# Attention with sigmoid scores on one core: four banks in the first sigmoid, a bank order from the middle outwards, and keys copied into their natural order

## The chip, the cores and the metric

One core of a Trainium2 chip runs the whole program. The time is the device time of one execution in microseconds (us); three executions were timed, and their median counts. One more execution was recorded by the hardware profiler; all durations below are from that one.

## What is computed

The input is x, 4 images of 64 channels by 96 x 96 pixels (N = 9216 pixels), in float32. Layer 0 normalises x in groups of two channels, makes queries and keys of 8 channels and values of 64, and adds an attention whose weights are sigmoids, not a softmax:

```python
energy = jnp.einsum('bcn,bcm->bnm', Q, K)
att = jax.nn.sigmoid(energy)
out = jnp.einsum('bcm,bnm->bcn', V, att).reshape(B, C, H, W)
out = out + x
...
scale = jax.nn.sigmoid(mlp(avg) + mlp(mx))
return out * scale[:, :, None, None]
```

Layer 1 normalises the result, takes its 2-D Fourier transform, mixes the channels of the 32 x 16 lowest modes with complex weights, and transforms back. Both layers add their input to their output. Four attention matrices of 9216 x 9216 are nearly all of the work.

## The kernel before

**Tiles.** The images are held as two pairs, `xs[0]` and `xs[1]`, with the 2 x 64 channels of a pair on 128 partitions. A pair's pixels are cut into 18 blocks of 512 queries (`NBLK`) and 72 chunks of 128 keys. A *tile* is the energies of 128 keys with 512 queries of one image; it fills one of the 8 banks of PSUM. A block has 144 tiles (`TILES`), the program 5184 (`ALL`). Tile i goes through three engines:

- TensorE (PE) multiplies 32 rows of `kT` (the keys, each split into a rounded high part and the rest so that one fp32r pass keeps the precision) with 32 rows of the block's queries (`energies`, L512). Tile i uses row group i % 4 of the array, so up to four of these matmuls run side by side. The stationary operand is 128 columns of `kT`. In `kT` the two halves h = 0, 1 of a block of keys lie interleaved, "(m h)", so these columns are every second element.
- ScalarE (ACT) takes the sigmoid of several neighbouring banks in one instruction and writes them to `at` in SBUF (`sigmoids`, L534).
- PE multiplies `at` with the values `vT` (`attend`, L551): float32, 64 columns of the array for each image of the pair, the two images side by side, accumulated over the 72 chunks in bank 7 or bank 0 (by the parity of the block).

**Bursts.** The tiles are worked in *bursts* of 7 (`SIZE`), or 6 where a bank is needed for something else. The planner (the `while len(done) < len(sizes)` loop) lists the bursts: 752 of them, 676 of 7 tiles, 74 of 6, one of 5 and one of 3. All banks but the accumulator belong to the burst, so there is no second set: the energies of the next burst go to the banks that the sigmoids of this one have read. `order[t]` is the list of banks of burst t in the order of its tiles, and the first `heads[t]` of them are read by its first sigmoid, the others by its second. Before the change `HEAD` is 3, and the order is 0 to 6 or 1 to 7, forwards or backwards by `way`.

**A step.** Step t of the main loop issues, in this order, on PE, ACT and DVE (whose order is written out by hand, `tc.manual_schedule`): the energies of burst t+1; a step of layer 1 that needs PE by itself, if one is due (`alone`; that burst has 6 tiles); the products of tiles that are left of burst t-1; the sigmoids of burst t+1; products of burst t; then, where one is due, the projections of `together[t]`; the rest of the products; then `ends[t]` (DMAs and small work on VectorE, DVE). The order on SyncE's queue (SP) and on GpSimd's (POOL) is the scheduler's.

**Projections.** `together` holds, in the first block of pair 0 (bursts 1 to 22), the projections of keys and values of the blocks that come next; in the last block of pair 0, those of pair 1; later `back_w` of layer 1. They use the banks that the first sigmoid of burst t+1 has just read, and the following burst has its order turned round (`way = -way`), so that its first energies use the other banks. `values_of(p, s)` (L446, 8 matmuls in two banks) gives values and also, in 32 more columns, queries and keys. On DVE it copies these 32 columns out (`u`, L460), then the values (`vT`, L451), then splits `u` into high and low parts (L471, L472, three times each) and transposes them (L474); four DMAs store the result in DRAM (L477).

**Where `kT` comes from.** For the first blocks (`DIRECT` = 7) `keys(0, s)` (L431, one bank) makes the keys a second time, straight in the layout of `kT`: DVE adds the bias (`full_k`, L410), rounds (`high_k`, L411) and writes `kT` (L420). For all other blocks `known_keys` (L484) reads the stored split from DRAM into `kT` with four DMAs on POOL's queue.

**Layer 1 of pair 0** runs beside the attention of pair 1, in the `alone` steps and the later `together` steps; the first two of them compute the channel gate (`hidden`, `gates`: DVE `gsum` L596, ACT `gate` L597). Layer 1 of pair 1 follows after the last burst. Neither is touched.

## Time and profile before

| | |
|---|---|
| three timed executions | 3073.45, 3070.55, 3075.11 us (median 3073.45) |
| profiled execution | 3069.26 us, of which the profile's span is 3067.5 us |
| granted TensorE clock | 0.997 |
| PE busy | 3045.5 us (99%) |
| ACT busy | 2418.7 us (79%) |
| DVE busy | 313.2 us (10%) |
| POOL busy | 84.4 us (3%) |
| products, L551 on PE | 11832 matmuls, 2401.8 us busy |
| energies, L512 on PE | 5184 matmuls, 571.9 us busy |
| sigmoids, L534 on ACT | 676 of four banks, 1.872 us each; 826 of three, 1.451 us each; one of two |

Stages by the table of windows (PE busy out of the stretch, in us): first block 94.75 of 98.80 (from 26.3), the other blocks of pair 0 up to the projections of pair 1 1278.67 of 1278.90 (from 125.1), those projections 120.90 of 121.00 (from 1404), attention of pair 1 with layer 1 of pair 0 824.64 of 825.00 (from 1525), attention of pair 1 alone 627.88 of 628.00 (from 2350), layer 1 of pair 1 80.63 of 89.00 (from 2978).

How to read it: PE is the row of matmuls, PEld that of the weight loads, which run beside the matmuls. PE counts as busy while a matmul is under way, also while it fills or drains, so 99% does not say that PE streams at its full rate; the distances between starts of instructions tell more. In a row of the timeline the first number is the start, the second the length, and the square bracket holds the idle time before it with what ended it. DVE and ACT may be idle without cost as long as nobody waits for them.

### The profile page before, as it was taken

Reading aid. Unit: us, or ns where it says so; the run is one execution under the profiler, and the core shown is the slowest. Engines: PE = TensorE matmul, PEld = TensorE weight load, DVE = VectorE, ACT = ScalarE, POOL = GpSimd, SP = SyncE. Lnnn points to the kernel's source line nnn. Section 1 sums busy time; section 2 is a strip of 40 time slices with the busy share of each in tenths; the row PEclk is TensorE's granted clock in tenths of the full one; section 3 lists DMA queues with packets and bytes.
Section 4 is the critical chain, followed back from the end, with each engine's and each line's share of the span. In section 5 each row is a group of like instructions: output and inputs, shape, how many; then the busy total and the mean of one; then the engine's idle time right before and its main releaser. Section 6 shows DMA issues by size and latency. Waiting matters only on the chain.

```text
span 3067.5 us, 43100 instructions
## 1 busy us (share of the span) xinstructions
PE 3045.5 (99%) x18772; PEld 1152.3 (38%) x18772; DVE 313.2 (10%) x731; ACT 2418.7 (79%) x1543; POOL 84.4 (3%) x168
## 2 busy tenths in 40 slices
PE   8999999999999999999999999999999999999998
PEld 4433333333333333334433333333333333333336
DVE  6300000000000000002411101000000000000005
ACT  4788888888888888887788887777778888888872
POOL 0200000000000000001200000000001000000001
PEclk9999999999999999999999999999999999999998
DMA  5100000000000000001322322321113000000027
GB/s 175 41 4 4 4 4 4 4 3 4 2 4 4 4 4 4 4 4 37 84 74 71 82 78 87 131 34 32 50 50 125 4 4 4 4 4 4 5 63 248
DMA packets 122285, 119.42 MB, mean 39 GB/s; under 512 B 83664, under 2 KB 93648, under 8 KB 122000
## 3 DMA queue, kind: packets, MB, share of 16 engines
q1 hardware_dynamic: 110080, 87.69, 10.1%
q0 software_dynamic: 9488, 24.26, 2.4%
q10 hardware_dynamic: 2528, 4.72, 0.4%
q8 instruction: 147, 2.41, 0.3%
q14 instruction: 42, 0.34, 0.0%
HBM read 80.50 MB, written 34.93 MB: 38 GB/s over the span
## 4 chain that ended last, share of the span: by engine, by line
PE 97%; DVE 1%; DMA 1%; issue 0%; ACT 0%; SPq 0%; POOL 0%; DVEq 0%; POOLq 0%; ACTq 0%
PE banks L551 75%; PE banks L512 17%; PE banks L446 1%; PE banks L209 1%; PE banks L379 1%; PE py L1003 0%; PE pv L209 0%; PE pa L905 0%; DMA x<-in_x_dram 0%; ACT at L534 0%; PE banks L357 0%; PE idle_I-15339_15354 L868 0%; SPq L477 0%; PE pu L917 0%; PE banks L305 0%
## 5 line engine op out<-in xcount | busy, mean ns | idle before, releaser
L534 ACT ACTIVATE at<-banks 128x1536 f32<-128x1536 f32 x1503 | 2396.0, 1640 | 559.3 <-PE banks L512 527.2
L551 PE MATMUL banks<-at,vT 128*64 128x512 f32 (+1 forms) x11832 | 2401.8, 546 | 0.0
L551 PEld LDWEIGHTS banks<-at,vT 128*64 128x64 f32 x11832 | 781.2, 136 | 1347.8 <-issue 1294.7
L512 PE MATMUL banks<-q,kT 32*128 32x512 f32 x5040 | 551.2, 458 | 0.5
L512 PEld LDWEIGHTS banks<-q,kT 32*128 32x128 f32 x5040 | 239.0, 190 | 450.5 <-ACT at L534 332.2
L557 DVE SCALAR_TENSOR_TENSOR x<-banks,x 128x512 f32<-128x512 f32 x36 | 24.9, 692 | 2006.0 <-PE banks L551 1930.7
L484 POOL DMA_DIRECT2D kT<-qk x116 | 57.4, 502 | 943.2 <-DMA qk<-turned 892.3
L446 PEld LDWEIGHTS banks<-cs,x 128*64 128x64 f32 x576 | 39.9, 139 | 17.0 <-issue 8.8
L446 PE MATMUL banks<-cs,x 128*64 128x160 f32 (+1 forms) x576 | 45.4, 299 | 0.0
L382 DVE TENSOR_TENSOR x<-banks,x 128x384 f32<-128x384 f32 x24 | 13.4, 557 | 196.6 <-PE banks L379 191.8
L149 POOL TENSOR_TENSOR mr_l<-ve_l,cs 128x1 f32<-128x1 f32 x4 | 2.2, 561 | 839.4 <-DVE ve_l L148 839.4
L559 DVE TENSOR_REDUCE maxs<-x 128x1 f32<-128x512 f32 x36 | 24.7, 686 | 1.2
L512 PE MATMUL banks<-q_first,kT 32*128 32x512 f32 x144 | 20.7, 475 | 4.1 <-DVE vT L451 2.4
L451 DVE TENSOR_TENSOR vT<-banks,cs 128x512 f32<-128x512 f32 x36 | 24.5, 680 | 0.0
L472 DVE TENSOR_TENSOR t<-u,t 128x64 fp32r<-128x64 f32 x105 | 23.5, 226 | 3.5
L656 DVE COPY ws<-banks 128x512 f32<-128x512 f32 x16 | 11.1, 692 | 116.3 <-PE banks L209 108.6
L565 DVE BATCH_NORM_STATS2 stats<-x 128x6 f32<-128x512 f32 x36 | 22.2, 679 | 5.7 <-DMA x<-in_x_dram 5.4
L474 DVE STREAM_TRANSPOSE turned<-t 128x384 f32<-128x384 f32 x35 | 20.7, 590 | 1.2
L890 POOL DMA_DIRECT2D x<-vT x3 | 2.7, 989 | 647.9 <-DVE less L880 647.9
L656 DVE COPY ae<-banks 128x512 f32<-128x512 f32 x6 | 4.1, 691 | 157.7 <-issue 115.6
L604 PE MATMUL banks<-x 128*128 128x256 f32 (+1 forms) x44 | 14.1, 470 | 5.8 <-DMA x<-in_x_dram 5.8
L379 PE MATMUL banks<-cs,ws 128*64 128x384 f32 x96 | 19.6, 486 | 0.0
(132 smaller groups left out, 447.8 us busy)
## 6 DMA issues: line engine op xcount, KB each, us to landing
ws<-in_spec_dram SPq DMA_DIRECT2D x20, 512.0 KB, 5.8
q<-qk SPq DMA_DIRECT2D x280, 32.0 KB, 1.8
x<-in_x_dram SPq DMA_DIRECT2D x14, 512.0 KB, 8.4
qk<-turned SPq DMA_DIRECT2D x140, 48.0 KB, 2.0
room<-in_spec_dram SPq DMA_DIRECT2D x12, 512.0 KB, 5.1
w<-in_spec_dram POOLq DMA_DIRECT2D x10, 512.0 KB, 6.8
old<-in_x_dram SPq DMA_DIRECT2D x12, 384.0 KB, 4.6
x1d<-x SPq DMA_DIRECT2D x12, 384.0 KB, 3.4
```

The source lines that it names most:

```text
L209: self.last = nc.tensor.matmul(pv[bass.ts(g, 32), :].rearrange("q (n k o) -> q n k o", n=SIDE, o=C)[:, :, k, :], self.ut[:, at:at + 32], s ...
L379: nc.tensor.matmul(py[bass.ts(b, C), :4 * W], self.z[:, i, bass.ts(b, C)], named("gw"), start=True, stop=True)
L446: projected[0] = nc.tensor.matmul(pp[bass.ts(e, P // 2), h, a, :], src[:, a, h, bass.ts(e, P // 2)], named("wv")[:, :width], start=True, s ...
L451: nc.vector.tensor_tensor(vT[:, 4 * s:4 * s + 4, :].rearrange("p (h a) m -> p h a m", h=2), pp[:, :, :, :P], named("bv").unsqueeze(1).unsq ...
L472: nc.vector.tensor_tensor(to[:, 1], whole, to[:, 0].bitcast(F32), ALU.subtract)
L484: nc.gpsimd.dma_start(kT[bass.ts(r, QK), s, :].bitcast(F32), split[p][s][:, r % 2, bass.ts(r // 2, NB // 2)])
L512: nc.tensor.matmul(banks[:, bank_of(i), :], kT[r:r + 32, i % TILES // 8, :].rearrange("r (m h) -> r h m", h=2)[:, i // 4 % 2], ask[i // TI ...
L534: nc.scalar.activation(at[:, of:of + n, :], banks[:, bank:bank + n, :], AF.Sigmoid)
L551: attended[0] = nc.tensor.matmul(acc[half, cols], vT[:, j, half], at[:, place(2 * pair + b), cols], start=(j == 0), stop=(j == NCH - 1 and ...
L557: nc.vector.scalar_tensor_tensor(blk, acc, 1.0, blk, ALU.mult, ALU.add, accum_out=sums[p][:, m:m + 1])
L559: mark[0] = nc.vector.tensor_reduce(maxs[p][:, m:m + 1], blk, AX.X, ALU.max)
L565: each = [lambda s=s: nc.vector.bn_stats(stats[:, s, :], xs[p][:, bass.ts(s, NB)]) for s in range(NBLK)]
```

## The change

- `HEAD` goes from 3 to 4: the first sigmoid of a burst takes four banks and the second the other three (two in a burst of 6). Where one to three banks of the burst are lent to projections (56 bursts), the first sigmoid keeps three.
- A new function `bank_order` puts four middle banks (3 to 6, or 4 to 7; mirrored where `way` is negative) first. `way` is turned only after projections, no longer set anew at the end of each block, so that the same banks come first before and after a block's end.
- `DIRECT` goes from 7 to 9: the keys of blocks 7 and 8 are projected by `keys`, too. `values_of(0, s)` is issued up to one burst earlier (`5 * SIZE` for `4 * SIZE`).
- `kT` is stored with the halves one after the other, "h m". `keys` writes `full_k` in that order. `known_keys` loads into a buffer `come`, and a DVE copy, two steps later (`arrive`), puts it into `kT`.
- In a step with projections DVE now empties the banks first (`full_k`, `u`, `vT`); rounding, splitting, the write to `kT` and the transpose follow behind the rest of the step's products (`rest`, `put_by`).

The number of bursts, their sizes and the steps with layer 1 stay as they were.

```diff
-SIZE, HEAD = 7, 3
-DIRECT = 7
+SIZE, HEAD = 7, 4
+DIRECT = 9
...
-        kT = kvp.tile([P, NBLK, NB // 2], F32R, tag="kT", name="kT")
+        kT = kvp.tile([P, NBLK, 2, P], F32R, tag="kT", name="kT")
...
-            ku, kh = halves(pp[:, :NB // 2], named("bk"), f"k_{p}_{s}")
-            low_or_high(kT[:, s, :], ku, kh, low_sb[:, 1:2])
+            shape = [P, NB // 2]
+            u = qp.tile(shape, F32, tag="turned", name=f"full_k_{p}_{s}")
+            nc.vector.tensor_scalar(u.rearrange("p (h m) -> p m h", h=2),
+                                    pp[:, :NB // 2].rearrange("p (m h) -> p m h", h=2),
+                                    named("bk"), None, ALU.add)
+
+            def rest():
+                h = qp.tile(shape, F32R, tag="t", name=f"high_k_{p}_{s}", bufs=1)
+                nc.vector.tensor_copy(h, u)
+                low_or_high(kT[:, s, :, :].rearrange("p h m -> p (h m)"), u, h, low_sb[:, 1:2])
+            return rest
...
         def known_keys(p, s):
 
+            come = work.tile([P, STRIP], F32, tag="old", bufs=2, name=f"come_{p}_{s}")[:, :NB // 2]
             for r in range(4):
-                nc.gpsimd.dma_start(
-                    kT[bass.ts(r, QK), s, :].bitcast(F32),
-                    split[p][s][:, r % 2, bass.ts(r // 2, NB // 2)])
+                nc.gpsimd.dma_start(come[bass.ts(r, QK), :],
+                                    split[p][s][:, r % 2, bass.ts(r // 2, NB // 2)])
+            return lambda: nc.vector.tensor_copy(
+                kT[:, s, :, :], come.rearrange("p (m h) -> p h m", h=2))
...
-                                 kT[r:r + 32, i % TILES // 8, :].rearrange(
-                                     "r (m h) -> r h m", h=2)[:, i // 4 % 2],
+                                 kT[r:r + 32, i % TILES // 8, i // 4 % 2, :],
...
+        def arrive(t, p, s):
+            come = []
+            end(t, lambda: come.append(known_keys(p, s)))
+            end(t + 2, lambda: come[0]())
...
+        def bank_order(few, odd, n):
+
+            if way < 0:
+                odd = not odd
+            if few:
+                a = [4, 5, 6, 3, 2, 1]
+            elif not odd:
+                a = [4, 5, 6, 3, 2, 1, 0]
+            elif 0 < n < HEAD:
+                a = [5, 6, 7, 4, 3, 2, 1]
+            else:
+                a = [4, 5, 6, 7, 3, 2, 1]
+            return a if way > 0 else [7 - bank for bank in a]
...
-            free = range(1, 7) if few else range(7) if block[t] % 2 == 0 else range(1, 8)
-            if crossing:
-                way = 1 if n % 2 else -1
-            elif together.get(t - 1):
+            if together.get(t - 1):
                 way = -way
-            heads.append(max(HEAD, sum(size for size, _ in together.get(t, ()))))
-            order.append(list(free)[::way][:ALL - total[t]])
+            beside = sum(size for size, _ in together.get(t, ()))
+            heads.append(HEAD - 1 if 0 < beside < HEAD else HEAD)
+            order.append(bank_order(few, block[t] % 2, beside)[:ALL - total[t]])
...
-                i = 0
+                i, put_by = 0, []
                 for size, step in together.get(t, ()):
+                    if size == 2 and i > 1:
+                        put_by.pop(0)()
                     spare[0] = min(order[t + 1][i:i + size])
                     i += size
+                    put_by += [step() or (lambda: None)]
+                attend(items[at_work:])
+                for step in put_by:
                     step()
-                attend(items[at_work:])
```

## The prediction

> **What bounds the kernel now.** I read the page's head first, then the chain, then the timeline burst by burst. Head and chain (share of the span by engine, then by line):

> ```profile
> span 3067.5 us, 43100 instructions
> PE 3045.5 (99%) x18772; PEld 1152.3 (38%) x18772; DVE 313.2 (10%) x731; ACT 2418.7 (79%) x1543; POOL 84.4 (3%) x168
> ...
> PE 97%; DVE 1%; DMA 1%; issue 0%; ACT 0%; SPq 0%; POOL 0%; DVEq 0%; POOLq 0%; ACTq 0%
> ```

> PE sets the end, DVE and ACT only where PE waits for them. The question is what a burst of 7 tiles takes and what sets that. I call the start of a burst's first key-weight load its start, and the distance to the next one its period. 604 of the 752 bursts have 7 tiles and nothing beside them; their median period is 3.829 us, and in sum they are only 9.5 us above 604 times that. So almost nothing is lost there, unless the 3.829 us themselves can shrink. One number tempts: ACT's two sigmoids take 3.22 us together and start 0.61 us after the burst, 3.83 in all; and the fourth key-weight load (its bank comes free with the second sigmoid) stands at 55 to 63 ns, not at 10. That is the wait which a first sigmoid of four banks removes. Two neighbouring bursts from the timeline of weight loads (start, length, idle before it):

> ```profile
> 304.47 0.32 PEld L512 LDWEIGHTS banks<-q,kT 32*128 32x128 f32 x7 [0.39 <-ACT at L534]
> 305.14 0.63 PEld L551 LDWEIGHTS banks<-at,vT 128*64 128x64 f32 x8 [0.36 <-issue]
> ...
> 308.30 0.31 PEld L512 LDWEIGHTS banks<-q,kT 32*128 32x128 f32 x7 [0.81 <-issue]
> 308.97 0.14 PEld L551 LDWEIGHTS banks<-at,vT 128*64 128x64 f32 x2 [0.36 <-issue]
> ```

> In the first the second sigmoid was done 108 ns early and the fourth load stood at 10 ns; in the second it stood at 62. Energies to products takes 0.67 us in both, and the periods are 3.832 and 3.828. The loads of the second round stand at 115 to 120 ns anyway, and behind them the wait disappears. The steady burst is PE's own: 7 x 0.427 = 2.99 us of products, 0.43 of energies, 0.41 of filling and draining at the two changes.

> **Part 1, four banks first: 0 in the steady burst.** One burst of before has a first sigmoid of four (its steps lend four banks): it starts at 628 ns, not 614. The second then ends at 0.628 + 3.22 = 3.85 us, 20 ns into the next burst; the fifth load gets its release near 70 ns, ahead of its 115. Gain 0, loss 0.

> **A real gain: late second sigmoids, -3.2.** After a burst of 6, two old tiles are left, and the second sigmoid of the next burst waits until PE has read their places in `at`:

> ```profile
> 297.28 1.45 ACT L534 ACTIVATE at<-banks 128x1536 f32<-128x1536 f32 x1 [0.60 <-PE banks L512]
> 298.94 1.88 ACT L534 ACTIVATE at<-banks 128x2048 f32<-128x2048 f32 x1 [0.21 <-PE banks L551]
> ...
> 300.87 0.20 PEld L512 LDWEIGHTS banks<-q,kT 32*128 32x128 f32 x4 [0.18 <-ACT at L534]
> ```

> It starts 2.27 us into its burst instead of 1.96, ends late, and holds four loads of the next burst until 376 ns; that period is 3.978. With four banks first the second sigmoid starts at 0.628 + 1.77 = 2.40, past the wait, and ends at 3.85. I count 15 such bursts at about 0.14 us and 14 at 0.08 (loads at 313 to 320): 3.2 us, between 0 and 3.6. Ten more at 0.25 us stay: there a full burst's sigmoids meet a period of only 3.40, and 3 or 4 banks first give the same end.

> **Bank order, `way`: 0.** Only at 4 places does a first sigmoid now wait for an old tile (at most 0.5 us each). A block's end in before shows DMA waits for the new queries (0.07 to 0.17 us each), which stay.

> **Natural order of `kT`: 0, bounds -6.8 and 0.** The nearest rows are loads of 128 columns with unit stride (L905, L868): their second load follows after 107 ns, that of `kT` (four loads at once) after 115 to 116. If all 9 ns were the stride, 751 x 9 ns = 6.8 us would go. I take 0: L446 loads every second element, too, and takes 139 ns against 137 of L379. [...]

> **Part 2, emptying banks first: +4.2.** The line-up of DVE in a step with both projections, before:

> ```profile
> 62.25 0.48 DVE L410 TENSOR_SCALAR full_k<-banks,cs 128x256 f32<-128x256 f32 x1 [0.83 <-issue]
> 62.77 0.29 DVE L411 CAST high_k<-full_k 128x256 fp32r<-128x256 f32 x1
> 63.09 0.48 DVE L420 SCALAR_TENSOR_TENSOR kT<-high_k,cs,full_k 128x256 fp32r<-128x256 f32 x1
> 63.50 0.28 DVE L460 TENSOR_TENSOR u<-banks,cs 128x128 f32<-128x128 f32 x1
> 63.70 0.68 DVE L451 TENSOR_TENSOR vT<-banks,cs 128x512 f32<-128x512 f32 x1
> ```

> `kT` is ready at 63.58, 4.66 us into its burst (start 58.92); the burst lasts 5.34 without waits (3.83 + 1.085 values + 0.43 keys). After the change, DVE takes `full_k`, waits for the values' matmuls (their end + 0.28 us, 4.24 us into the burst), takes `u` and `vT` (0.21 + 0.68), then L411 and L420 (0.8): `kT` at 5.86 + 0.06, or 0.43 more where the projections come half a pair later. The very next burst needs these keys, at tile 4, 5, 6, 0, 1, 2, 3 for blocks 2 to 8. A wait of L costs L at tiles 0 to 2, and L - 0.24 from tile 3 on (the loads held until 1287 and 2094 ns in before cost 1.05 and 1.87). Against the waits that stand there in before: +0.57, +0.30, +0.58, +0.83, +0.58, +1.01, +0.34 = 4.2. What the early emptying frees is covered by these same waits. Bounds 0 (if the order hid itself) and 7 x 1.0.

> **Part 3, `come` copies: +5.65.** In the built instruction order the copy stands on DVE behind the transpose of step t + 2. With values alone, `u` begins 3.85 or 4.25 us into the burst in turn, the transpose ends 2.6 later, and the copy (0.29 as L411, 0.48 as L410; I take 0.3) is done and seen at `u` + 2.9: 6.75 or 7.15, where the next burst starts at 4.92. Blocks 9, 10, 11 are used by just that next burst (tiles 4, 5, 6): waits of 2.25, 1.85, 2.25, less 0.24: 2.0 + 1.65 + 2.0. From block 12 on, a burst more lies between, and the copy is early. Bounds 0 and 3 x 2.4. The 18 copies of pair 1 (some 15 bursts ahead) cost PE nothing; if that cover went, 0.3 us each.

> **DMA waits that go: -4.95.** In before, keys of block 7 and on arrive late by DMA:

> ```profile
> 83.43 0.31 PEld L512 LDWEIGHTS banks<-q_first,kT 32*128 32x128 f32 x5 [0.39 <-ACT at L534]
> 84.90 0.38 PEld L512 LDWEIGHTS banks<-q_first,kT 32*128 32x128 f32 x2 [1.17 <-DMA kT<-qk]
> ```

> Against its undisturbed 4.92 (with values) or 3.83, bursts 8, 11, 14, 17, 18 are longer by 0.36, 1.43, 0.82, 0.98, 1.27, three others by 0.03 each. Block 7 becomes direct, the copies replace 9 to 11, and from 12 on the values come a burst earlier: the chain from the transpose's end to the landed keys (91.7 to 100.6, 8.9 us: SP's four DMAs, then POOL's four) is over before the copy's turn, by about 1 us. Bounds -4.95 and -2.95 (that hand lost on the last bursts).

> **Two more key projections: +0.86** (2 x 0.43 on PE).

> **The gate, +1.7.** The last two copies of pair 1 stand on DVE ahead of `gsum`, which ACT's `gate` and every sigmoid behind it wait for:

> ```profile
> 1518.27 1.96 POOL L484 DMA_DIRECT2D kT<-qk  x4 [2.73 <-PE banks L551]
> 1520.40 0.16 DVE L596 TENSOR_REDUCE gsum<-banks 128x1 f32<-128x2 f32 x1 [6.82 <-PE banks L593]
> ```

> The last of these four DMAs lands near 1521.8, so `gsum` moves from 1520.4 to about 1522; bounds 0 and 2.5. [...]

> **Sum**: -3.2 + 4.2 + 5.65 - 4.95 + 0.86 + 1.7 = +4.3 us. On the profiled execution 3069.26 becomes 3073.5; on the median, 4.2 above it, 3073.45 becomes **3077.7**, 0.14% longer. About 0.2% (6.1 us) is what a measurement of this kernel tells from no change: below 3067.3 is faster, above 3079.6 slower.

> **Rivals.** (a) *The fourth load paces the burst after all.* ACT's 3.83 equals the period, which speaks for it; the pair at 304 and 308 speaks against. Up to 50 ns x 604 = 30 us: 3047. (b) *Slower: DVE's queue waits for DMAs.* A copy that is not landed holds the next `u` and `vT`. It decides once the chain of 8.9 us exceeds about 11.8 (9.8 for two steps, 2 until the next `u`); then each of some 23 copies costs the excess, 0.6 us each being 14: 3090. POOL's issues of 0.5 us and the two `come` buffers speak for it, the 1 us in hand against. (c) *The first block's waits go without the new ones* (DVE less late than I sum): -4.95 + 0.86 - 3.2 = -7.3: 3066. That the steady state doesn't change at all is my forecast.

> **How the numbers follow.** Forecast 0.60 (0.40 within 0.2%, 0.20 slower, for its bounds reach +14.6); (a) 0.10, faster; (b) 0.15, slower; (c) 0.15 (0.09 faster, 0.06 within). Faster 0.19, same 0.46, slower 0.35. The low bounds of all terms sum to -6.8 - 3.6 - 4.95 + 0.86 = -14.5 (3059), the high ones to 7 + 7.2 - 2.95 + 0.86 + 2.5 = +14.6 (3088). This range leaves out (a) and half of (b), about 0.18.

> **What would show it.** Right: periods of plain bursts stay at 3.83, loads of bursts 10 to 12 wait for DVE's `kT` copy near 2 us, bursts 6 and 7 for the `kT` that L411 of the changed kernel writes, second sigmoids no longer wait for PE at 300 us, `gsum` starts behind the last `come` copy. Wrong: a plain period below 3.82, or bursts 14 to 18 still waiting.

## The result and the profile after

The changed kernel takes 3073.31 us (median of 12 executions, 3071.9 to 3075.25), the kernel before, timed beside it, 3072.89 us (12 executions, 3068.29 to 3075.11). The ratio is 1.0003, with a 95% interval of 0.9994 to 1.0011: no change that this measurement can tell. In us the interval is -1.8 to +3.4; the median of 3077.7 us that was forecast, 4.2 us above that of before, was not met. The profiled execution took 3073.33 us with a span of 3071.2, where that of before took 3069.26 with 3067.5. Head and chain of the page after:

```profile
span 3071.2 us, 43088 instructions
PE 3040.2 (99%) x18780; PEld 1137.4 (37%) x18780; DVE 323.6 (11%) x764; ACT 2412.0 (79%) x1543; POOL 80.9 (3%) x160
...
PE 96%; DVE 2%; ACT 1%; DMA 1%; issue 0%; SPq 0%; POOL 0%; DVEq 0%; ACTq 0%; POOLq 0%
```

PE is 5 us less busy in a span that is 3.7 us longer, and DVE now ends some of its waits (2% of the chain for 1%). So the change gained and lost at once. Summed by kinds of burst from the starts of the first key-weight loads, after less before, in us (a plain burst is one with nothing beside it):

| part of the span | bursts | after less before |
|---|---|---|
| first block (bursts 0 to 21) | 22 | +7.55 |
| plain bursts, no wait in either | 545 | -4.20 |
| bursts with a wait in before (late second sigmoids, last bursts of a block) | 57 | -4.42 |
| bursts with a wait only in after | 5 | +1.08 |
| bursts behind a block's end or beside layer 1 | 95 | -1.75 |
| projections of pair 1 (355 to 377) | 23 | +0.55 |
| the gate (378 to 381) | 4 | +4.49 |
| ahead of burst 0 and behind the last | | +0.43 |
| sum | | +3.73 |

The plain burst, from the timeline of weight loads of the changed kernel (start, length, idle before it):

```profile
300.43 0.31 PEld L518 LDWEIGHTS banks<-q,kT 32*128 32x128 f32 x6 [0.39 <-issue]
...
303.82 0.30 PEld L518 LDWEIGHTS banks<-q,kT 32*128 32x128 f32 x7 [0.38 <-issue]
...
307.64 0.30 PEld L518 LDWEIGHTS banks<-q,kT 32*128 32x128 f32 x7 [0.81 <-ACT at L539]
```

The median period of plain bursts is 3.822 us where it was 3.829. The fourth load now stands at 10 ns (56 before), the fifth at 108 (116 before). The loads from 300.43 on wait for no late sigmoid any more.

In the first block the copies hold the keys, as the prediction had it. Weight loads of bursts 10 and 11 of the changed kernel:

```profile
85.82 0.19 PEld L518 LDWEIGHTS banks<-q_first,kT 32*128 32x128 f32 x4 [0.81 <-issue]
87.97 0.19 PEld L518 LDWEIGHTS banks<-q_first,kT 32*128 32x128 f32 x3 [1.96 <-DVE kT L491]
92.64 0.29 PEld L518 LDWEIGHTS banks<-q_first,kT 32*128 32x128 f32 x5 [0.39 <-issue]
94.36 0.18 PEld L518 LDWEIGHTS banks<-q_first,kT 32*128 32x128 f32 x2 [1.43 <-DVE kT L491]
```

DVE's line-up in the step of burst 5 (to be read beside the one in the prediction) has turned round: the values first, then `kT`. The copy of `full_k` alone also takes 0.69 us instead of 0.48; it now changes the order of the columns (in the run without copies, below, where it does not, it takes 0.48 again).

```profile
60.45 0.69 DVE L427 TENSOR_SCALAR full_k<-banks,cs 128x256 f32<-128x256 f32 x1 [2.50 <-PE banks L422]
61.47 0.29 DVE L460 TENSOR_TENSOR u<-banks,cs 128x128 f32<-128x128 f32 x1 [0.34 <-PE banks L446]
61.68 0.68 DVE L451 TENSOR_TENSOR vT<-banks,cs 128x512 f32<-128x512 f32 x1
62.28 0.28 DVE L433 CAST high_k<-full_k 128x256 fp32r<-128x256 f32 x1
62.60 0.48 DVE L411 SCALAR_TENSOR_TENSOR kT<-high_k,cs,full_k 128x256 fp32r<-128x256 f32 x1
```

At the gate, `gsum` starts behind the last copy, 6.5 us later in the span and 2.6 us later within its burst:

```profile
1526.71 0.29 DVE L491 CAST kT<-come 128x256 fp32r<-128x256 f32 x1 [5.56 <-DMA come<-qk]
1526.91 0.15 DVE L601 TENSOR_REDUCE gsum<-banks 128x1 f32<-128x2 f32 x1
```

One thing stood in no step of the prediction. The table of windows of the changed kernel, cut at the times at which the granted clock changes (length, busy time and number of PE, PEld, DVE, ACT, POOL, then the granted clock, DMA share, GB/s):

```profile
53.24:56.65 3.41, 2.04 (x15) 0.96 (x15) 3.17 (x14) 1.51 (x2) 0.00 (x0) 1.00 0.13 26
56.65:60.06 3.41, 3.41 (x12) 1.20 (x10) 1.30 (x3) 1.82 (x1) 0.00 (x0) 0.50 0.34 78
...
1527.79:1531.21 3.42, 2.03 (x13) 0.82 (x13) 3.37 (x5) 3.42 (x3) 0.00 (x0) 1.00 0.86 295
1531.21:1534.62 3.41, 3.41 (x10) 0.97 (x8) 1.88 (x3) 1.99 (x2) 0.00 (x0) 0.50 0.86 297
```

Twice PE waited for about 1.4 us of a window of 3.41 us, and twice the next window ran at half clock. PE is "busy" through all of it, at half the pace: in the first of these half-clock windows the pairs of weight loads of the products begin 0.85 us apart (56.85 and 57.70), in plain bursts 0.43. Burst 5 lasts 9.88 us, of which some 1.7 are this. The first of the two waits is not new. In burst 5 the last loads wait for the copy of the values (L451) out of the banks, until 2.09 us into the burst here and 2.10 in before, and before has 1.46 us of idle PE in one window there, without a half-clock window behind it. The loads of after, then the loads and that window of before:

```profile
55.41 0.18 PEld L518 LDWEIGHTS banks<-q_first,kT 32*128 32x128 f32 x2 [1.80 <-DVE vT L451]
...
53.80 0.20 PEld L512 LDWEIGHTS banks<-q_first,kT 32*128 32x128 f32 x4 [1.90 <-DVE vT L451]
...
50.26:53.68 3.42, 1.96 (x23) 1.26 (x19) 3.17 (x12) 1.36 (x1) 0.00 (x0) 1.00 0.19 45
```

### The profile page after: what moved, and what is told of

Same layout as the page of the kernel before. It is cut to its first block, busy times and chain, and to the rows that moved or that the text cites. A ratio compares the mean times of both kernels' runs of the same rounds, so it can differ in the third digit from the quotient of the medians.

```text
span 3071.2 us, 43088 instructions
## 1 busy us (share of the span) xinstructions
PE 3040.2 (99%) x18780; PEld 1137.4 (37%) x18780; DVE 323.6 (11%) x764; ACT 2412.0 (79%) x1543; POOL 80.9 (3%) x160
## 4 chain that ended last, share of the span: by engine, by line
PE 96%; DVE 2%; ACT 1%; DMA 1%; issue 0%; SPq 0%; POOL 0%; DVEq 0%; ACTq 0%; POOLq 0%
PE banks L556 75%; PE banks L518 16%; PE banks L446 1%; ACT at L539 1%; PE banks L209 1%; PE banks L379 1%; PE py L1029 0%; PE pv L209 0%; DMA x<-in_x_dram 0%; PE pa L931 0%; PE banks L357 0%; PE idle_I-15399_15414 L894 0%; DVE vT L451 0%; PE pu L943 0%; PE banks L305 0%
## 5 line engine op out<-in xcount | busy, mean ns | idle before, releaser
L539 ACT ACTIVATE at<-banks 128x2048 f32<-128x2048 f32 (+1 forms) x1503 | 2389.2, 1640 | 587.1 <-PE banks L518 560.1
L518 PE MATMUL banks<-q,kT 32*128 32x512 f32 x5040 | 542.8, 452 | 4.1 <-ACT at L539 3.9
L518 PEld LDWEIGHTS banks<-q,kT 32*128 32x128 f32 x5040 | 223.8, 182 | 451.4 <-issue 325.7
L562 DVE SCALAR_TENSOR_TENSOR x<-banks,x 128x512 f32<-128x512 f32 x36 | 24.9, 692 | 1994.5 <-PE banks L556 1994.5
L489 POOL DMA_DIRECT2D come<-qk x108 | 53.8, 505 | 951.0 <-DMA qk<-turned 896.7
L446 PEld LDWEIGHTS banks<-cs,x 128*64 128x64 f32 x576 | 40.0, 139 | 16.3 <-issue 11.2
L446 PE MATMUL banks<-cs,x 128*64 128x160 f32 (+1 forms) x576 | 45.4, 299 | 0.0
L451 DVE TENSOR_TENSOR vT<-banks,cs 128x512 f32<-128x512 f32 x36 | 24.5, 680 | 0.0
L474 DVE CAST t<-u 128x64 fp32r<-128x64 f32 x105 | 19.6, 189 | 0.2
```

The costliest lines, as they stand in the source:

```text
L446: projected[0] = nc.tensor.matmul(pp[bass.ts(e, P // 2), h, a, :], src[:, a, h, bass.ts(e, P // 2)], named("wv")[:, :width], start=True, s ...
L451: nc.vector.tensor_tensor(vT[:, 4 * s:4 * s + 4, :].rearrange("p (h a) m -> p h a m", h=2), pp[:, :, :, :P], named("bv").unsqueeze(1).unsq ...
L489: nc.gpsimd.dma_start(come[bass.ts(r, QK), :], split[p][s][:, r % 2, bass.ts(r // 2, NB // 2)])
L518: nc.tensor.matmul(banks[:, bank_of(i), :], kT[r:r + 32, i % TILES // 8, i // 4 % 2, :], ask[i // TILES][r:r + 32, :], start=True, stop=True)
L539: nc.scalar.activation(at[:, of:of + n, :], banks[:, bank:bank + n, :], AF.Sigmoid)
L562: nc.vector.scalar_tensor_tensor(blk, acc, 1.0, blk, ALU.mult, ALU.add, accum_out=sums[p][:, m:m + 1])
```

## The experiments

Each run is compared with executions of the kernel before that were timed beside it on the same chip; their medians were 3069.72 to 3070.13 us, where that of the result is 3072.89, so ratios are to be compared, not times. "First block" is the sum of bursts 0 to 21 from the run's trace, 110.28 us before and 117.83 after.

Each trace is of one execution, and the waits for keys out of DRAM differ from one execution to the next. The run with stalls, below, has the same code up to burst 29 as the run with both edits, and yet its first block took 110.22 us for 111.93: burst 8 took 5.18 us for 6.09, burst 11 4.91 for 6.40, burst 15 6.42 for 4.91, while bursts 2 to 7 agree to 0.01 us. So a difference of 1 to 2 us in bursts of the first block that wait for DMAs is not shown by one pair of traces.

### Four banks first, alone

The kernel before with `HEAD = 4` and `bank_order`:

```diff
-SIZE, HEAD = 7, 3
+SIZE, HEAD = 7, 4
...
-            heads.append(max(HEAD, sum(size for size, _ in together.get(t, ()))))
-            order.append(list(free)[::way][:ALL - total[t]])
+            beside = sum(size for size, _ in together.get(t, ()))
+            heads.append(HEAD - 1 if 0 < beside < HEAD else HEAD)
+            order.append(bank_order(few, block[t] % 2, beside)[:ALL - total[t]])
```

> The kernel before with the four-bank first sigmoid and the middle-out bank order alone (keys, their storage, DVE's order and the DMAs as before). Theory A (the prediction): the steady burst is PE's own, so plain bursts keep their 3.829 us though the fourth load now stands at 10 ns, the fifth stays at 115 to 116, and only the late second sigmoids go: about -3.0 us, some 3070 us, with nothing lost in the first block. Theory B: the fourth load at 10 ns instead of 56 is what made plain bursts of the changed kernel 7 ns shorter: period 3.822 here, -5 more, about -8 us, 3065. Either way the step of the gate (bursts 378 to 380) shows whether four banks first cost something there by themselves: about +1.5 us by the first sigmoid that stood at 2.2 us in the changed kernel, 0 if all of that loss comes from the copies.

3067.33 us, ratio 0.9992 (0.9983 to 1.0000). Two neighbouring plain bursts of this run:

```profile
302.74 0.31 PEld L512 LDWEIGHTS banks<-q,kT 32*128 32x128 f32 x7 [0.81 <-ACT at L534]
...
306.57 0.32 PEld L512 LDWEIGHTS banks<-q,kT 32*128 32x128 f32 x7 [0.39 <-issue]
```

The fourth load stands at 10 ns in the median, the fifth at 115, and the median period is 3.830: theory A holds, theory B is out. Bursts that waited in before lose 4.09 us, those behind a block's end or beside layer 1 another 0.98; five bursts with new waits take back 1.09 and the projections of pair 1 0.75: -3.2 us. The gate costs 1.25 us by itself, as the changed kernel's first sigmoid at 2.2 us into burst 378 had hinted. Contrary to both theories, the first block grew by 1.99, of which 1.68 are a half-clock window in burst 5.

### Unit stride, alone

The kernel before with chunks of neighbouring pixels; the same in the split and in DRAM, and no copy:

```diff
-        src = xs[p][:, bass.ts(s, NB)].rearrange("p (a m h) -> p a h m", a=2, h=2)
+        src = xs[p][:, bass.ts(s, NB)].rearrange("p (a h m) -> p a h m", a=2, h=2)
...
-                    split[p][s].rearrange("r k (a g m) -> g r (k a) m", a=2, g=4)[g],
-                    turned[bass.ts(g, QK)].rearrange("r k a m -> r (k a) m"))
+                    split[p][s].rearrange("r k (a h g m) -> g r (k a h) m", a=2, h=2, g=4)[g],
+                    turned[bass.ts(g, QK)].rearrange("r k a (h m) -> r (k a h) m", h=2))
...
-                                 kT[r:r + 32, i % TILES // 8, :].rearrange(
-                                     "r (m h) -> r h m", h=2)[:, i // 4 % 2],
+                                 kT[r:r + 32, i % TILES // 8, bass.ts(i // 4 % 2, P)],
```

> The kernel before with three banks first, and unit stride in kT got without any copy: a chunk is 128 neighbouring pixels, in the values, in the split and in kT (the transposed split is stored in DRAM in runs of 32 elements instead of 64). Theory A (the prediction): the stride of the key weights costs nothing, plain bursts stay at 3.829 and the time at about 3073. Theory B': unit stride takes 7 to 8 ns from the second round of key-weight loads (fifth load at 108 instead of 116), and from every burst: period 3.822, some 715 bursts, -5 us, about 3068. The finer runs in DRAM can make the keys of blocks 7 and on land later in the first block: 0 to +2 us.

3064.57 us, ratio 0.9982 (0.9973 to 0.9991). The row of the key-weight loads among the costliest groups of before, then of this run; the last number ahead of the second bar is the mean length of one in ns:

```profile
L512 PEld LDWEIGHTS banks<-q,kT 32*128 32x128 f32 x5040 | 239.0, 190 | 450.5 <-ACT at L534 332.2
...
L512 PEld LDWEIGHTS banks<-q,kT 32*128 32x128 f32 x5040 | 228.1, 182 | 450.9 <-ACT at L533 323.8
```

With four banks first it is 190 ns as well. The fourth load still stands at 60 ns, the fifth at 108, the period is 3.822: theory B' holds, -4.29 us in the 550 plain bursts and -1.3 in the others behind the first block. The first block is 0.37 us longer (burst 8 alone +0.53); that the finer runs in DRAM delay its keys is not shown, since that burst differs by 0.91 us between two executions of the same code.

### Both

> Both of the former edits on the kernel before, without the late splits, the copies and the two more key projections. If the terms add up: -3.0 (late second sigmoids) and -5.0 (unit stride) and 0 to +2 (finer runs in DRAM, gate), so about 3066 us, faster than both kernels; plain period 3.822. If the fourth load and the stride share one limit, no more than the better of the two alone.

3062.21 us, ratio 0.9976 (0.9967 to 0.9985): faster than both kernels. The terms add up: plain bursts -4.25, bursts that waited -4.40, the gate +1.23, the first block +1.65 (no half clock in it; 1.04 of it is burst 19, whose loads wait for sigmoids that started only 3.3 us into burst 18, the second with four banks first behind bursts with three).

### Splitting at once

The changed kernel with the rest of each projection issued right behind its first copies:

```diff
-                    put_by += [step() or (lambda: None)]
+                    (step() or (lambda: None))()
+                    put_by.append(lambda: None)
```

> The changed kernel, with the rest of each projection (rounding, the write to kT, splitting, transposing) issued on DVE right behind its first copies, as before the change; copies by way of come, nine direct blocks and unit stride stay. The prediction's term for the emptying is 4.2 us, all of it in bursts 2 to 8, where kT waits for the values: by it about 3069 us, and bursts 2 to 8 together 4 to 6 us shorter than in the changed kernel (46.69 us), with bursts 10 to 12 unchanged (6.83, 6.39, 6.83). Rival: the keys are late because the queue of DVE is full there in either order, and no more than 1 us comes back.

3069.92 us, ratio 1.0001 (0.9992 to 1.0010), so by time alone nothing can be told. By the traces the rival (no more than 1 us comes back) is out: bursts 2 to 9 take 47.28 us, not 51.86: 4.58 less, of which 1.7 are the half clock of burst 5 that is not there, and 2.9 the emptying. But bursts 10 to 12 take 21.78 instead of 20.04, because here burst 10 is the one that ran at half clock:

```profile
80.50:83.91 3.41, 1.76 (x13) 0.58 (x11) 2.92 (x11) 1.45 (x1) 0.00 (x0) 1.00 0.16 35
83.92:87.33 3.41, 3.41 (x14) 1.24 (x11) 0.00 (x0) 1.88 (x1) 1.96 (x4) 0.50 0.47 96
```

### No copy

The changed kernel with unit stride by the layout, as above, and keys loaded straight into `kT`:

```diff
-            come = work.tile([P, STRIP], F32, tag="old", bufs=2, name=f"come_{p}_{s}")[:, :NB // 2]
             for r in range(4):
-                nc.gpsimd.dma_start(come[bass.ts(r, QK), :],
-                                    split[p][s][:, r % 2, bass.ts(r // 2, NB // 2)])
-            return lambda: nc.vector.tensor_copy(
-                kT[:, s, :, :], come.rearrange("p (m h) -> p h m", h=2))
+                nc.gpsimd.dma_start(
+                    kT[bass.ts(r, QK), s, :, :].rearrange("p h m -> p (h m)").bitcast(F32),
+                    split[p][s][:, r % 2, bass.ts(r // 2, NB // 2)])
+            return lambda: None
```

> The changed kernel without the copies: chunks of neighbouring pixels as in the unit-stride run, keys loaded by DMA straight into kT; four banks, nine direct blocks and late splitting stay. The prediction put the copies at +5.65 us in bursts 10 to 12 and +1.7 at the gate; the trace of the changed kernel has waits of 2.16, 1.72 and 2.16 us there, and gsum 2.6 us late and, in the very next window, a half clock that cost some 1.7 us more. Theory: without the copies bursts 10 to 12 last some 4.9 us each (5 to 5.6 us less in sum), bursts 378 to 380 lose only what four banks first cost there (1.3 us, as in both runs with four banks on the kernel before), no half clock behind the gate; 0 to +2 us come back as DMA waits because the runs in DRAM are finer. About 3065 where the changed kernel would be at 3070 on this chip. Rival: without the copy the waits for the DMAs of before come back in full (4.95 us), and the time stays within 2 us of the changed kernel.

3062.78 us, ratio 0.9977 (0.9968 to 0.9986). Bursts 10 to 12 take 15.01 us (20.04 with the copies), with waits of no more than 0.2 us:

```profile
89.45 0.57 PEld L515 LDWEIGHTS banks<-q_first,kT 32*128 32x128 f32 x7 [0.39 <-issue]
94.51 0.46 PEld L515 LDWEIGHTS banks<-q_first,kT 32*128 32x128 f32 x7 [0.81 <-issue]
```

So the copies cost 5.0 us there. The gate costs 1.23 us instead of 4.49, and no half clock follows it: the copies' share is 3.26, of which 1.7 are the half clock and some 1.55 the late `gsum`. The rival (DMA waits come back in full) is out.

### Values early, on the fast kernel; three banks behind projections

On the run with both edits, first the values one burst earlier, then also three banks first in the two bursts behind values:

```diff
-                while (valued < min(NBLK, (total[t] + 4 * SIZE - 1) // 8 + 1)
+                while (valued < min(NBLK, (total[t] + 5 * SIZE - 1) // 8 + 1)
...
             beside = sum(size for size, _ in together.get(t, ()))
+            if any(sum(size for size, _ in together.get(t - k, ())) > 1 for k in (1, 2)):
+                beside = max(beside, 1)
```

> Four banks and unit stride on the kernel before, and the values issued up to one burst earlier, as in the change, with seven direct blocks and no copies. The prediction's term for DMA waits that go was -4.95, of which the changed kernel showed -0.8, -1.0, -0.6 at bursts 14, 17, 18. Theory: an earlier burst of values takes bursts 11, 14, 17 and 18 of the run with both edits (6.41, 5.70, 4.45 and 5.31 us) to 4.9, 4.9, 3.9 and 4.5: -3 to -4 us, about 3058 to 3059. Rival: SP's queue of stores (23 us without a pause in that run) is what makes the keys late, and an earlier start moves the waits to other bursts: within 1 us of that run.

> The run before this one, with three banks first in the two bursts behind each step with values (seven bursts change, two of them at the gate, bursts 377 and 378, the others in the first block). In all kernels with four banks first the first sigmoid of burst 378 waits to 2.2 us into its burst until PE has read its places in at; with three it stood at 0.67. Theory: bursts 377 to 380 come back to the 18.9 us of the kernel before, 1.3 us less, and the first sigmoid of the burst behind the projections of the first block stands at about 0.65, not at 1.4 to 3.3: -1.3 to -2 us in all. Rival: the second sigmoid waits instead, and nothing changes.

3061.90 us, ratio 0.9971 (0.9959 to 0.9983), and 3061.72 us, 0.9972 (0.9961 to 0.9983). Earlier values leave bursts 11, 14 and 18 at 4.91, 4.95 and 3.82 us, at or below what their theory had, and burst 17 at 4.88, where 3.9 was expected. The first block is 3.56 us shorter than in the trace of the run with both edits, but only 1.84 shorter than in that of the run with stalls, which has the same code there, so the size of the gain is not shown; 1.27 are lost again in the bursts with `back_w`, where the bank order comes out mirrored, and the times cannot tell the run from that with both edits (ratio 0.9976): the 3058 to 3059 us of the theory were not reached. The second run is a miss: burst 378 falls from 4.46 to 3.82 us, but 379 to 381 grow from 11.47 to 13.35, with first sigmoids at 2.0 and 2.6 us into bursts 379 and 380; in the first block burst 17 gains 1.05 and bursts 19 and 20 lose 1.75. It is not the second sigmoid that waits, as its rival had it, but the first one of the first bursts with four banks behind those with three: the wait moves with that border, and nothing is won.

### Stalls on purpose

The run with both edits, and in 43 plain bursts of pair 0 one tile's sigmoid made 1 to 6 times more:

```diff
+                    for _ in range(dose.get(t + 1, 0)):
+                        of, bank, _ = next(parts(t + 1))
+                        nc.scalar.activation(at[:, of, :], banks[:, bank, :], AF.Sigmoid)
                     sigmoids(t + 1)
```

> The run with both edits, with stalls put in on purpose: in 43 plain bursts of pair 0 ACT makes the sigmoid of the burst's first tile 1 to 6 times more ahead of its two sigmoids (7 or 8 bursts for each number, some 0.6, 1.1, 1.6, 2.1, 2.6 and 3.1 us). Theory: PE waits that long, and in addition, where PE is idle for more than some 1.35 us of one of the 3.41 us windows on which the granted clock changes, the next window runs at half clock and costs another 1.7 us: none of the 22 short stalls, some 60% at 1.6, 75% at 2.1, all above 2.6, so about 25 half windows and 75 + 43 us in all, near 3175 us. Rival: the half clock at burst 5 and at the gate is not due to PE's waits: no half windows here beyond those of that run, near 3135 us.

One execution: 3183.37 us. By the number of extra sigmoids:

| extra sigmoids | stalls | PE idle, us | followed by half clock | time lost, without / with half clock, us |
|---|---|---|---|---|
| 1 | 8 | 0.19 | 0 | 0.46 / - |
| 2 | 7 | 0.81 | 0 | 1.09 / - |
| 3 | 7 | 1.37 | 2 | 1.72 / 3.42 |
| 4 | 7 | 2.00 | 4 | 2.33 / 4.07 |
| 5 | 7 | 2.60 | 7 | - / 4.57 |
| 6 | 7 | 3.27 | 7 | - / 5.60 |

The theory holds, the rival (3135 us, no half windows) is out; 20 half windows came where about 25 were expected. The half-clock windows begin at whole multiples of 3.413 us from each other. What decides in these stalls is how much of one falls into a single window. Two stalls of four extra sigmoids, each with 2.0 us of idle PE, in the table of windows:

```profile
685.95:689.36 3.41, 1.41 (x11) 0.38 (x7) 0.00 (x0) 3.41 (x3) 0.00 (x0) 1.00 0.00 0
689.37:692.77 3.40, 3.40 (x11) 1.01 (x10) 0.00 (x0) 2.65 (x2) 0.00 (x0) 0.50 0.00 0
883.92:887.33 3.41, 2.43 (x12) 0.57 (x8) 0.00 (x0) 3.31 (x4) 0.00 (x0) 1.00 0.00 0
887.33:890.74 3.41, 2.40 (x15) 0.98 (x17) 0.00 (x0) 3.41 (x4) 0.00 (x0) 1.00 0.00 0
890.75:894.15 3.40, 3.40 (x27) 1.36 (x25) 0.00 (x0) 2.25 (x2) 0.00 (x0) 1.00 0.00 0
```

The first lies in one window, and the next has half clock; the second is split 0.98 to 1.01 over two, and nothing follows. Of the stalls whose largest share of a window was 1.32 us or less (22) none was followed by half clock, of those with 1.37 or more (21) all but one (at 1.46).

### No copy and splitting at once

The changed kernel with the edits of both runs ("both undone" in what follows): what stays are four banks, bank order, unit stride, nine direct blocks and the earlier values.

> The changed kernel without the copies (as in the run without copies) and without the late splits (as in the run with splits at once): what stays of the change is four banks first, the bank order, unit stride by the layout, nine direct blocks and the earlier values. If the two terms add up: bursts 2 to 9 as in the run with splits at once (2.9 us less than in the changed kernel, half clocks aside), bursts 10 to 12 at about 5 us each as in the run without copies, the first block some 2 us shorter than before, no half clock behind burst 5; about 3059 to 3060, the fastest so far. Rival: with the splits back at once, the stores of the split start earlier but the values' banks are free later, and the two cancel: the time of the run without copies, 3062.8.

3058.83 us, ratio 0.9961 (0.9947 to 0.9975), the fastest here. The first block takes 107.14 us, no half clock lies in the attention, and DVE's share of the chain is back at 1%:

```profile
span 3057.1 us, 43055 instructions
...
PE 97%; DVE 1%; ACT 1%; issue 0%; DMA 0%; SPq 0%; POOL 0%; DVEq 0%; ACTq 0%
```

The first block of five kernels, in us (half-clock windows in brackets):

| bursts | before | after | no copy | split at once | both undone |
|---|---|---|---|---|---|
| 0, 1 | 7.35 | 7.54 | 7.34 | 7.53 | 7.34 |
| 2 to 9 | 45.87 | 51.86 (1) | 51.87 (1) | 47.28 | 46.49 |
| 10 to 12 | 15.16 | 20.04 | 15.01 | 21.78 (1) | 14.94 |
| 13 to 21 | 41.91 | 38.39 | 38.38 | 38.39 | 38.37 |
| sum | 110.28 | 117.83 | 112.61 | 114.99 | 107.14 |

### Stride four

The changed kernel with the keys of two neighbouring blocks interleaved in `kT`, 16 bytes from column to column:

```diff
-        kT = kvp.tile([P, NBLK, 2, P], F32R, tag="kT", name="kT")
+        kT = kvp.tile([P, NBLK // 2, P, 2, 2], F32R, tag="kT", name="kT")
...
-                                 kT[r:r + 32, i % TILES // 8, i // 4 % 2, :],
+                                 kT[r:r + 32, i % TILES // 16, :, i // 8 % 2, i // 4 % 2],
```

> The changed kernel with the keys of two neighbouring blocks interleaved in kT as well, so that the 128 columns of a chunk stand 16 bytes apart (every fourth element) instead of next to each other; the copies on DVE write them so. Only plain bursts are to be read (the bookkeeping of waits sees two blocks as one, so the first block and the projections of pair 1 may lose some us). Theory: a key-weight load takes longer with the stride, 7 to 9 ns for each doubling: fifth load at 122 to 125 ns, plain period 3.836 to 3.840, 11 us or more on the whole. [...] Rival: the gain of unit stride comes from something else in that layout (the values' loads, the banks): plain period 3.822 as in the changed kernel.

One execution: 3168.22 us. Loads of a plain burst and the group's row:

```profile
1254.70 0.54 PEld L520 LDWEIGHTS banks<-q,kT 32*128 32x128 f32 x7 [0.39 <-issue]
```

```profile
L520 PEld LDWEIGHTS banks<-q,kT 32*128 32x128 f32 x5040 | 400.7, 313 | 447.6 <-issue 304.2
```

The fifth load stands at 212 ns and the period is 3.947, so neither the theory (122 to 125 ns, 3.836 to 3.840) nor the rival (3.822) holds. What a doubling of the distance costs is not one number: the fifth load comes 8 ns later from one element to two, and 96 ns later from two to four; a load takes 182 ns on average in the changed kernel (one element), 190 in before (two) and 313 here (four).

| distance of the columns | fifth load, ns | period, us |
|---|---|---|
| 1 element | 108 | 3.822 |
| 2 elements | 116 | 3.829 |
| 4 elements | 212 | 3.947 |

## Why the prediction came out as it did

The forecast of no measurable change held. On the pair of profiled executions even the size fits: +4.3 us was summed, they differ by 4.07. But that fit is in good part luck. The timed medians differ by 0.42 us only, and in the traces two errors took each other away: a gain that was put at 0 and two windows of half clock that were in no term.

- **Four banks first: right in the steady burst and for the late sigmoids.** 0 in the steady burst, with the fourth load at 10 ns and no change (first run), so rival (a) is out. In that run the 24 bursts that no longer wait for a late second sigmoid gave 2.9 us, where 3.2 were summed.
- **Bank order and block ends, 0: wrong on both sides.** In the same run the 33 last bursts of a block, whose waits were to stay, gave 3.2 us; why they got shorter no run separates. On the other side 11 bursts grew by 2.3 us, the projections of pair 1 by 0.75 and the gate by 1.25. That all but the gate nets to some -3 us, like the term for the sigmoids alone, is luck.
- **Natural order of `kT`, 0: wrong.** It gave 4.2 us in the plain bursts, 5.6 in all when done alone. The bounds held the value, the choice within them did not. I had the right nearest row (second loads with unit stride, at 108 to 109 ns in the trace, not 107 as I wrote) and set it aside for one that is farther: L446 has the stride and takes no longer. In the unit-stride run L446 takes 139 ns with unit stride as well, so that row says nothing against a gain: its loads have 64 columns, on all rows of the array at once, and are not four on four row groups. The claim that the steady burst is PE's own was right and too short: the rate at which key weights come in is part of it (8 ns at the fifth load, 7 in the period). Its products stand 0.429 us apart in the trace of before, 3.00 for seven, where 0.427 and 2.99 were taken; the split of the rest into energies, filling and draining was an estimate, which no run takes apart.
- **Emptying banks first, +4.2: right in kind, somewhat large.** 2.9 us (after against split at once) and 3.7 (no copy against both undone), half clocks left out. The waits for the `kT` of L411 stand in bursts 4, 7, 8 and 9 (loads at 921, 490, 922 and 490 ns); in burst 6 they are only 39 ns, since burst 5 ran long. The slower `full_k` (0.69 for 0.48 us) was not in the sum: it adds 0.2 us to each of bursts 2, 4 and 6 in the run with splits at once, where that of both undone has none.
- **`come` copies, +5.65: right.** The loads waited until 2155, 1721 and 2155 ns, where 2.25, 1.85 and 2.25 us were worked out; 5.0 us.
- **DMA waits that go, -4.95: right, somewhat large.** Without copies, bursts 11, 14, 17 and 18 are 1.28, 0.78, 0.99 and 0.64 us shorter than before, 3.7 in all; by what was said of waits for DMAs, this size holds for one pair of executions. What stays in burst 18 is another wait: its loads at 873 ns follow a sigmoid of the burst ahead that started late, at 1425 ns.
- **Two more key projections, +0.86: right where it can be read.** Burst 7 of the run with both undone is 0.42 longer; in burst 8 a wait of before is gone as well.
- **The gate, +1.7: too small.** 4.49. The late `gsum` was there, 2.6 us later within its burst where 1.6 were worked out: SP's first load of `old` (384 KB) waits for the first of the two last copies to free its buffer, is issued at 1521.18, and the last store of the split, under way since, landed only at 1522.5. The cost of the late `gsum`, some 1.55, is near the term. Missing were 1.2 us by four banks first (I had counted 0.5 us at most for such places) and 1.7 us of half clock.
- **Not in the sum: the clock.** Two half-clock windows, 3.4 us, are the other error; in the profiled execution they took away most of what unit stride gave. The one at the gate follows a wait that the change made: it is in two of the three traces of kernels with the copies and in none without them. The one behind burst 5 follows a wait that before has, too, so it cannot be put down to the change. In eleven of the twelve traces PE is idle in burst 5 for 1.24 to 1.57 us of one window. A half window followed at 1.24, 1.36, 1.36 and 1.37, and none at 1.30, 1.36, three times 1.37, 1.46 (before) and 1.57. What decides there stays open.

Of the rivals, (b) did not come: DVE waits 24.9 us in all for the DMAs of six copies, but none of the 35 `u` waits behind one, and PE pays only at the gate. (c) is what the run with both undone became: 107.14 for 110.28 in the first block.

How many half windows the timed executions had, no trace tells. Their mean clock says that it matters: the 32 executions of before beside the first four runs took 3065.9 us on average at a mean clock of 0.998 (4 of them), 3068.6 at 0.997 (12), 3071.3 at 0.996 (15) and 3076.8 at 0.995 (1); the 27 others took 3069.1 (3), 3068.8 (10), 3071.2 (12) and 3074.8 (2). That a profile of before without any half-clock window in the attention was compared with one of after that had two may be why the profiles differ by 4.07 us and the medians by 0.42; this is argued, not shown.

## What to carry over

In the run with stalls, a stall of PE had two prices: its own length, and 1.7 us more where enough of it (1.37 us or more, in 20 of 21) fell into one window of the clock. Four extra sigmoids, 2.0 us of idle PE, cost 2.33 us or 4.07. When a layout gives a gain, look for a way to get it without new instructions: here another choice of which keys make up a chunk gave unit stride with no copy on DVE, and the copies and the late splits had cost what the layout and the four banks brought. And where bounds are far apart, take the value by the row that has the same shape, not by the one that agrees with the rest of the story.
